# Group norm, shifted-window attention and depthwise convolution on one core: every engine's instructions in written order, softmax split in two, convolution taps written one by one, another prologue

## The chip, the cores and the metric

The kernel runs on one core of a Trainium2 chip. The metric is the device time of one execution in microseconds (us). Three runs of the kernel before gave 5260.55, 5266.62 and 5267.27 us; the median is 5266.62 us. The profile is of a further execution, of 5283.2 us from its first to its last instruction, and all times within the run are read from it.

## The reference

All data are float32. The input x has 16 images of 56 x 56 pixels and 384 channels, and there are two layers with residuals:

```python
x = x + attention(gn(x), w_qkv, w_out, b_out, rel_pos_table)
x = x + depthwise3x3(gn(x), sign(w))      # w clipped, then binarised
```

`gn` normalises each image over 32 groups of 12 channels, so its mean and variance need the whole image. `attention` rolls the image by three rows and columns, cuts it into 8 x 8 windows of 7 x 7 tokens, computes q, k and v (12 heads of 32), a softmax over 49 keys with a position bias and, in the last row and column of windows, a mask, and multiplies by `w_out`. The convolution has nine taps per channel and zero padding. The second `gn` needs all of an image's first layer before the convolution of that image can begin.

## The kernel before

**Tiling.** A strip `s` is one row of eight windows, 7 rows by 56 columns, kept as channels by tokens in three blocks of 128 channels (`NC` = 3); an image has 8 strips (`NS`), the run 128. Half a strip, four windows, is a unit `u`; there are 256. A unit's softmax tile `t` has 128 partitions by 24 rows of 49 scores.

**Loops.** The main loop runs over the units. Each has heavy work on TensorE: an even unit computes the next strip's q and k (`query_key`, six groups of matmuls, L288) and the first third of the previous strip's output (`project`, L401); an odd unit computes the next strip's `value` (four groups, L301), calls `normalize` for the strip after it (ScalarE writes `xn`, L277) and does the other two thirds of `project`. Between them stand `transpose` (three, L358, of the softmaxed scores `e`) and `attend` (L379). At the head of each unit stands `softmax(u + 1)`: the scores (`ps`, L323), then VectorE's scale and bias (L334), maximum (L344), subtraction (L345), ScalarE's `exp` (L347), and VectorE's sum, reciprocal and product (L349, L351, L352).

**Light work.** A table `side` holds other work with due times in units: `fetch` and `load` of the next image (transposes `pl`, L261; ScalarE copy L264; `bn_stats`, L268), the `gn` chain (`norm_gather`, `norm_scale`: statistics to DRAM and back, GpSimd arithmetic, coefficients to DRAM and back, all on GpSimd's DMA queue), `center`, and the convolution of the previous image: `band` (DMA of 16 rows, `xb`), `depthwise` (ScalarE writes the padded, normalised band `hp`, L461, and the centre tap `o`, L475; VectorE adds eight taps, L486) and `store` (transposes `px`, L498; ScalarE copy L499; DMA). An image has four bands of three channel blocks, so twelve depthwise steps, spaced 1.3 units (1.1 for image 14).

**What sets the order.** Only TensorE keeps the order in which the code is written; the other engines are ordered by a scheduler with priorities, which moves the vector part of `softmax` ahead by `SOON`. `issue_after` holds an image's first padded band back until a recent `exp` has been issued.

**Buffers.** All matmul outputs but the scores share a ring of four PSUM banks (`bank`); a new group of matmuls waits until the copy or addition that empties the bank's last use is done. The scores have one buffer of their own. There are two `xb`, two `hp` and five `o` tiles, and eleven strips `x`.

**Before and after the main loop.** The prologue loads and transposes the weights, then the bias table and the depthwise weights, then image 0, strip after strip, with two load buffers `xl`; then its `gn` chain, q and k, and the first scores. After the last unit only the `gn` chain and the convolution of image 15 are left.

Of the kernel before, what the change touches and what calls it, by code (L numbers as in the profile page):

```python
# [33 lines left out]
def kernel(  # L34
# [35 lines left out]
    SOON = 700  # L70
# [6 lines left out]
    xpool = ctx.enter_context(tc.tile_pool(name="x", bufs=11))  # L77
# [7 lines left out]
    hpool = ctx.enter_context(tc.tile_pool(name="hp", bufs=2))  # L85
# [11 lines left out]
    for c in range(NC):  # L97
        nc.scalar.dma_start(bo_sb[:, c : c + 1], b_out[c * P : (c + 1) * P].unsqueeze(1))
    power = const.tile([P, 1], F32, tag="power", name="power")
    nc.gpsimd.memset(power, -0.5)  # L100
# [7 lines left out]
    nc.gpsimd.memset(xn, 0.0)  # L108
    nc.gpsimd.memset(qk[:, :, ST:], 0.0)

    xls = [const.tile([P, NL, C], F32, tag=f"xl{n}", name=f"xl{n}") for n in range(2)]
    for xl in xls:
        nc.gpsimd.memset(xl[:, NL - 1, :], 0.0)

    es = [const.tile([P, NH, 2, HT], F32, tag=f"e{n}", name=f"e{n}") for n in range(2)]
    for e in es:
        nc.gpsimd.memset(e, 0.0)

    def load_weights():
        for dst, src in ((wq_t, w_qkv), (wo_t, w_out)):  # L120
            for r in range(src.shape[0] // P):
                wl = io.tile([P, LG, C], F32, tag="io", name="wl")
                nc.scalar.dma_start(wl[:, 0, :], src[r * P : (r + 1) * P, :])
                pw = bank("pw")
                for c in range(NC):
                    nc.tensor.transpose(pw[:, c * P : (c + 1) * P], wl[:, 0, c * P : (c + 1) * P], ident)
                nc.vector.tensor_copy(
                    dst[:, :, r * P : (r + 1) * P], pw[:, : NC * P].rearrange("p (c q) -> p c q", c=NC)
                )

    def load_depthwise():
        wl = [io.tile([P, LG, C], F32, tag="io", name=f"dwl{n}")[:9, 0, :] for n in range(3)]
        nc.scalar.dma_start(wl[0], w_dw.rearrange("a b c o -> (a b) (c o)"))

        nc.vector.tensor_scalar(wl[1], wl[0], -1.0, 1.0, ALU.max, ALU.min)
        nc.vector.tensor_scalar(wl[0], wl[1], 0.0, None, ALU.is_gt)
        nc.vector.tensor_scalar(wl[2], wl[1], 0.0, None, ALU.is_lt)
        nc.vector.tensor_tensor(wl[0], wl[0], wl[2], ALU.subtract)
        nc.vector.tensor_tensor(wl[0], wl[0], wl[1], ALU.subtract)
        nc.vector.tensor_tensor(wl[0], wl[0], wl[1], ALU.add)  # L140
        pw = bank("pdw")
        for c in range(NC):
            nc.tensor.transpose(pw[:, c * 9 : (c + 1) * 9], wl[0][:, c * P : (c + 1) * P], ident[:9, :9])
        nc.vector.tensor_copy(dw_t, pw[:, : NC * 9].rearrange("p (c t) -> p c t", c=NC))

    def load_bias():

        rel = io.tile([P, LG * C], F32, tag="io", name="rel")[:, : T * NH]
        nc.gpsimd.memset(rel, 0.0)
        flat = rel.rearrange("q (a n) -> q a n", a=WIN)  # L150
        for q in range(T):
            qr, qc = divmod(q, WIN)
            first = (WIN - 1 - qr) * REL + (WIN - 1 - qc)
            row = rel_table[first : first + 1, :]
            src = bass.AP(
                tensor=row.tensor,
                offset=row.offset,
                ap=[[NH, 1], [REL * NH, WIN], [1, WIN * NH]],
            )
            (nc.gpsimd if q % 2 else nc.scalar).dma_start(flat[q : q + 1], src)  # L160
        nc.gpsimd.dma_start(flat[HT : HT + T], flat[0:T])
        mask = io.tile([P, LG * C], F32, tag="io", name="mask")[:, : 2 * T].rearrange("q (v k) -> q v k", v=2)
        nc.gpsimd.memset(mask, 0.0)
        for w in range(2):
            nc.gpsimd.dma_start(mask[w * HT : w * HT + T], wmask[0:T, :, 0:T])
        rel_n = rel.rearrange("q (k j i) -> q i j k", j=NC, i=HPC)
# [13 lines left out]
    def norm_gather(key):  # L180
# [9 lines left out]
        nc.gpsimd.dma_start(by_channel.rearrange("(c p) k -> p c k", p=P), mv)  # L190
        gt = small.tile([GROUPS, GS, 2], F32, tag="gt", name=f"gt{name}")
        nc.gpsimd.dma_start(gt.rearrange("g n k -> g (n k)"), by_channel.rearrange("(g n) k -> g (n k)", n=GS))
        parts[key] = gt

    def norm_scale(key):
# [30 lines left out]
        nc.gpsimd.dma_start(by_channel.rearrange("(g n) k -> g (n k)", n=GS), both.rearrange("g n k -> g (n k)"))  # L226
        coef = small.tile([P, NC, 2], F32, tag="coef", name=f"coef{name}", bufs=4)
        nc.gpsimd.dma_start(coef, by_channel.rearrange("(c p) k -> p c k", p=P))
# [43 lines left out]
    recent = []  # L272
# [39 lines left out]
    def softmax(u):  # L312
# [3 lines left out]
        for j in range(NC):  # L316
            for w in range(2):
                for r in range(2):
                    for i in range(HPC):
# [9 lines left out]
                        )  # L329

        with tc.high_priority(offset=SOON):
            n = NC * 2 * T
            t = two.tile([P, HPC * n], F32, tag="t", name=f"t_{u}", bufs=1)
            nc.vector.scalar_tensor_tensor(  # L334
                t.rearrange("q (i n) -> q i n", i=HPC),
                pp[:, :, :n],
                QSCALE,
                bias[:, int(s % NS == NS - 1)].rearrange("q (i j) w k -> q i (j w k)", i=HPC),
                ALU.mult,
                ALU.add,  # L340
            )
            tr = t.rearrange("q (n k) -> q n k", k=T)
            top = small.tile([P, 2 * NH], F32, tag="top", name=f"top_{u}")
            nc.vector.tensor_reduce(top, tr, AX.X, ALU.max)  # L344
            nc.vector.tensor_tensor(tr, tr, top.unsqueeze(2).to_broadcast([P, 2 * NH, T]), ALU.subtract)  # L345
            e = es[u % 2].rearrange("q h w k -> q (h w) k")[:, :, :T]
            recent[:] = [nc.scalar.activation(e, tr, AF.Exp)]  # L347
            total = small.tile([P, 2 * NH], F32, tag="total", name=f"total_{u}")
            nc.vector.tensor_reduce(total, e, AX.X, ALU.add)  # L349
            inv = small.tile([P, 2 * NH], F32, tag="inv", name=f"inv_{u}")  # L350
            nc.vector.reciprocal(inv, total)  # L351
            nc.vector.tensor_tensor(e, e, inv.unsqueeze(2).to_broadcast([P, 2 * NH, T]), ALU.mult)  # L352
# [99 lines left out]
    def depthwise(b, k, c):  # L452
        coef, cen = coefs[1, b], centers[b]
        xb, rows, at, n = bands.pop((b, k, c))
        hp = hpool.tile([P, BR + 2, W + 2], F32, tag="hp", name=f"hp_{b}_{k}_{c}")
        nc.gpsimd.memset(hp[:, :, 0 : W + 2 : W + 1], 0.0)
# [4 lines left out]
        padded = lambda: nc.scalar.activation(  # L461
# [6 lines left out]
        if k == 0 and c == 0 and recent:  # L468

            with tc.issue_after(recent[0].ins):  # L470
                padded()
        else:
            padded()
# [5 lines left out]
            bias=cen[:, c, 1:2],  # L479
            scale=cen[:, c, 0:1],  # L480
        )
        for t in range(9):
            if t == 4:
                continue
            dy, dx = divmod(t, 3)
            nc.vector.scalar_tensor_tensor(  # L486
                acc, hp[:, dy : dy + BR, dx : dx + W], dw_t[:, c, t : t + 1], acc, ALU.mult, ALU.add
            )
        outs[b, k, c] = acc

# [20 lines left out]
    def plan_conv(p, first, step):  # L511

        at(first, norm_gather, (1, p))
        at(first + 0.7, norm_scale, (1, p))
        at(first + 1.2, center, p)
        for n in range(NB * NC):
            k, c = divmod(n, NC)
            when = first + 1.5 + step * n
            at(max(when - min(step, 1.2), first), band, p, k, c)
            at(when, depthwise, p, k, c)  # L520
        for k in range(NB):
            tiles = -(-BR * W // OT // LG)
            for g in range(tiles):
                at(first + 1.5 + step * NC * (k + 1 + 0.7 * g / tiles) + 0.1, store, p, k, g)

    def plan_load(b):

        for r in range(NS):
            when = NU * (b - 1) + max(1.7 + 1.3 * r, 2 * r - 3)
            at(when - 0.7, fetch, b * NS + r)  # L530
            for c in range(NC):
                at(when + 0.8 * c / NC, load, b * NS + r, c)
        at(when + 0.7, norm_gather, (0, b))
        at(when + 1.5, norm_scale, (0, b))
# [22 lines left out]
    with tc.manual_schedule(engines={mybir.EngineType.PE}):  # L557
        load_weights()
        load_bias()
        load_depthwise()  # L560
        fetch(0)
        for s in range(NS):
            if s + 1 < NS:
                fetch(s + 1)
            for c in range(NC):
                load(s, c)
        norm_gather((0, 0))
        norm_scale((0, 0))
        normalize(0)
        run([(query_key, (0, m)) for m in range(2 * NC)])  # L570
        softmax(0)
        run([(value, (0, n)) for n in range(2 * UPS)])
        normalize(1)
        for b in range(1, B):
            plan_load(b)
            plan_conv(b - 1, NU * b + 1, 1.3 if b < B - 1 else 1.1)
        for u in range(B * NU):
            todo = heavy(u)
            light = [(w, f, a) for w, f, a in sorted(side.pop(u, []), key=lambda i: i[0])]
            if u + 1 < B * NU:  # L580
                softmax(u + 1)
            slots = len(todo)
            n = 0
            for i, (f, args) in enumerate(todo):
                f(*args)
                if i < NC:
                    transpose(u, i)
                elif i == NC:
                    attend(u)
# [3 lines left out]
            for i in range(len(todo), NC + 1):  # L593
                if i < NC:
                    transpose(u, i)
                else:
                    attend(u)
# [3 lines left out]
        recent.clear()  # L601
        plan_conv(B - 1, B * NU, 1.0)
        for u in sorted(side):
            for _, g, a in sorted(side[u], key=lambda i: i[0]):
                g(*a)
# [44 lines left out]
```

## Time and profile before

| stretch of the run | us | what it is |
|---|---|---|
| 0 to 120.6 | 120.6 | prologue, up to the first scores |
| 120.6 to 393 | 272.5 | image 0: attention, loads of image 1, no convolution |
| 14 images (1 to 14) | 315.7 to 320.9 each, mean 317.6 | attention, loads of the next image, convolution of the one before |
| image 15 up to its last scores, 5121.4 | 272 for 7 strips | attention and convolution, no loads |
| 5121.4 to 5283 | 162 | end of attention, `gn` chain, convolution of image 15 |

The stretches are found from the starts of the score matmuls (L323), 96 of which begin each unit. Over the whole span TensorE is busy for 4740.4 us in matmuls, VectorE for 3871.1, ScalarE for 2332.7, GpSimd for 532.4. Some mean durations: a softmax pass of VectorE 1368 to 1383 ns (five for each unit; the scaling with bias is one), the reciprocal 298, a tap 1022, `exp` 1208, an addition into `y` 562 and its statistics 563, a padded band 1116, a centre tap 1054. In these lists a row gives the instruction's line, engine and operation, output and inputs, how often it ran, its busy time and mean, and how long the engine was idle just before it, with what released it.

### The profile page before, as it was taken

How to read it: one execution, taken by the hardware profiler on the slowest of the kernel's cores; microseconds unless marked ns; L12 is line 12 of the kernel's file. 1: busy time of each engine (PE TensorE's matmuls, PEld its weight loads, DVE VectorE, ACT ScalarE, POOL GpSimd, SP SyncE). 2: the span in 40 equal slices, each digit the busy share in tenths (PEclk: the TensorE clock that was granted, in tenths of full speed). 3: DMA queues.
4: the chain of work that ended last, by engine and by line, in shares of the span. 5: the costliest groups of instructions: out<-in, count | busy, mean ns of one | idle time of the engine just before them, and what ended most of it. 6: DMA issues, size and time to landing. Idle time of an engine off the chain costs nothing. (4 is left out here: it accounts for less than half of the span.)

```text
span 5283.2 us, 145019 instructions
## 1 busy us (share of the span) xinstructions
PE 4740.4 (90%) x65127; PEld 3023.6 (57%) x65127; DVE 3871.1 (73%) x4371; ACT 2332.7 (44%) x4417; POOL 532.4 (10%) x1386
## 2 busy tenths in 40 slices
PE   4999989989898998989989899999989999899981
PEld 2665656556565655656556565555656556565551
DVE  2557678777786787778777786777778777787777
ACT  1434435444443544445444444444445444444432
POOL 2001010111101011010111101010010101101000
PEclk9999999999999999999999999999999999999995
DMA  2112212122221212212122221222212122221113
GB/s 66 34 35 55 74 51 81 53 71 71 64 71 53 77 60 68 72 51 80 55 71 68 61 74 55 74 61 70 72 51 77 58 72 68 56 74 51 60 52 91
DMA packets 166078, 337.64 MB, mean 64 GB/s; under 512 B 22304, under 2 KB 124201, under 8 KB 165456
## 3 DMA queue, kind: packets, MB, share of 16 engines
q1 hardware_dynamic: 139008, 244.10, 17.5%
q0 software_dynamic: 23920, 81.82, 4.6%
q8 instruction: 511, 8.37, 0.7%
q10 hardware_dynamic: 2528, 2.44, 0.2%
q14 instruction: 111, 0.91, 0.1%
HBM read 169.69 MB, written 158.47 MB: 62 GB/s over the span
## 5 line engine op out<-in xcount | busy, mean ns | idle before, releaser
L288 PE MATMUL pq<-xn,wq_t 128*128 128x392 f32 x4608 | 1724.0, 515 | 100.4 <-ACT qk L295 77.9
L486 DVE SCALAR_TENSOR_TENSOR o<-hp,dw_t,o 128x784 f32<-128x784 f32 x1536 | 1532.8, 1022 | 293.6 <-ACT o L475 287.5
L288 PEld LDWEIGHTS pq<-xn,wq_t 128*128 128x128 f32 x4608 | 850.1, 196 | 621.5 <-ACT qk L295 88.3
L301 PE MATMUL pv<-wq_t,xn 128*128 128x384 f32 x3072 | 1100.6, 495 | 19.2 <-ACT v L309 16.7
L401 PE MATMUL py<-ot,wo_t 128*128 128x392 f32 x2304 | 832.5, 506 | 18.1 <-ACT v L309 8.7
L295 ACT COPY qk<-pq 128x392 f32<-128x392 f32 x768 | 369.5, 481 | 869.9 <-PE pq L288 869.9
L301 PEld LDWEIGHTS pv<-wq_t,xn 128*128 128x128 f32 x3072 | 543.0, 190 | 309.5 <-ACT v L309 27.4
L409 DVE TENSOR_TENSOR y<-py,x 128x392 f32<-128x392 f32 x384 | 215.8, 562 | 589.0 <-PE py L401 580.5
L401 PEld LDWEIGHTS py<-ot,wo_t 128*128 128x128 f32 x2304 | 430.6, 193 | 311.7 <-issue 15.1
L358 PEld LDWEIGHTS pp<-ident,e 113*128 113x128 f32 x3072 | 371.2, 142 | 258.7 <-issue 155.5
L347 ACT ACTIVATE e<-t 128x1176 f32<-128x1176 f32 x256 | 309.2, 1208 | 452.0 <-DVE t L345 451.8
L349 DVE TENSOR_REDUCE total<-e 128x24 f32<-128x1176 f32 x256 | 352.0, 1375 | 183.8 <-ACT e L347 183.8
L309 ACT COPY v<-pv 128x384 f32<-128x384 f32 x512 | 241.1, 471 | 499.4 <-PE pv L301 499.2
L498 PE MATMUL px<-ident,o 128*112 128x128 f32 x1344 | 225.5, 297 | 249.1 <-ACT qk L295 112.0
L461 ACT ACTIVATE hp<-xb,coef 128x896 f32<-128x896 f32 (+1 forms) x192 | 214.4, 1116 | 505.1 <-POOL coef L437 215.0
L358 PE MATMUL pp<-ident,e 113*128 113x113 f32 x3072 | 429.2, 262 | 3.9 <-DVE e L352 3.3
L334 DVE SCALAR_TENSOR_TENSOR t<-ps,bias 128x1176 f32<-128x1176 f32 x256 | 350.8, 1370 | 93.8 <-PE ps L323 93.8
L364 ACT COPY pt<-pp 128x392 f32<-128x392 f32 x768 | 374.8, 488 | 16.8 <-PE pp L358 16.5
L379 PEld LDWEIGHTS po<-pt,v 49*32 49x32 f32 x24576 | 254.4, 106 | 188.7 <-issue 81.2
L323 PEld LDWEIGHTS ps<-qk 32*64 32x64 f32 x24576 | 282.4, 131 | 136.1 <-issue 86.7
L352 DVE TENSOR_TENSOR e<-e,inv 128x1176 f32<-128x1176 f32 x256 | 353.9, 1383 | 5.7
L345 DVE TENSOR_TENSOR t<-t,top 128x1176 f32<-128x1176 f32 x256 | 352.9, 1379 | 4.7
(73 smaller groups left out, 3653.2 us busy)
## 6 DMA issues: line engine op xcount, KB each, us to landing
mid<-y POOLq DMA_DIRECT2D x112, 619.5 KB, 4.6
out_dram<-xo SPq DMA_DIRECT2D x192, 336.0 KB
xb<-mid SPq DMA_DIRECT2D x96, 472.0 KB
xb<-mid SPq DMA_DIRECT2D x96, 442.5 KB
xl<-in_x_dram SPq DMA_DIRECT2D x112, 288.0 KB
xl<-in_x_dram SPq DMA_DIRECT2D x112, 216.0 KB
out_dram<-xo SPq DMA_DIRECT2D x64, 168.0 KB
xl<-in_x_dram SPq DMA_DIRECT2D x48, 144.0 KB
```

Of the source, the lines that this page charges most:

```text
L288: nc.tensor.matmul(pq[:, :ST].rearrange("p (w t) -> p w t", t=T), wq_t[:, c, m * P : (m + 1) * P], xn[:, c, :, :T], start=(c == 0), stop=( ...
L295: nc.scalar.copy(qk[:, m, :ST], pq[:, :ST])
L301: nc.tensor.matmul(pv[:, :C], xn[:, c, 2 * n : 2 * n + 2].rearrange("p w t -> p (w t)"), wq_t[:, c, 2 * C : 3 * C], start=(c == 0), stop=( ...
L334: nc.vector.scalar_tensor_tensor(t.rearrange("q (i n) -> q i n", i=HPC), pp[:, :, :n], QSCALE, bias[:, int(s % NS == NS - 1)].rearrange("q ...
L345: nc.vector.tensor_tensor(tr, tr, top.unsqueeze(2).to_broadcast([P, 2 * NH, T]), ALU.subtract)
L347: recent[:] = [nc.scalar.activation(e, tr, AF.Exp)]
L349: nc.vector.tensor_reduce(total, e, AX.X, ALU.add)
L352: nc.vector.tensor_tensor(e, e, inv.unsqueeze(2).to_broadcast([P, 2 * NH, T]), ALU.mult)
L358: nc.tensor.transpose(pp[:, i * P : i * P + QT], es[u % 2][:QT, i * NC + j].rearrange("q w k -> q (w k)"), ident[:QT, :QT],)
L364: nc.scalar.copy(pt, pp.rearrange("k (n q) -> k n q", q=HT)[:, :, :T])
L401: nc.tensor.matmul(py[:, :ST], wo_t[:, c, m * P : (m + 1) * P], ots[s][:, c, :], start=(c == 0), stop=(c == NC - 1),)
L486: nc.vector.scalar_tensor_tensor(acc, hp[:, dy : dy + BR, dx : dx + W], dw_t[:, c, t : t + 1], acc, ALU.mult, ALU.add)
```

## The change

Every engine now takes its instructions in written order (`manual_schedule()` without a list of engines), so that the place of each call in the code is its place in the engine's queue. To fit this, `softmax` is split: `scores(u + 1)` with the scaling, maximum and subtraction stays at the head of the unit; the new `softmax(u + 1)`, `exp` and what follows it, is written after the fourth group of heavy work and ahead of `attend`. `depthwise` is split into `pad`, `middle` and eight calls of `tap`, each with its own due time an eighth of a step apart. The `hp` tiles become two fixed ones, zeroed once, so the column memsets go. The convolution starts `lead` = 3 units after the `gn` chain is begun (1.5 before). `plan_load` has new times, and `x` has twelve buffers. The prologue fetches two strips first, stages all weights in `x` buffers, loads image 0, and transposes the weights while the `gn` chain is under way; the bias rows all go on GpSimd's DMA queue. The `gn` chains of image 0 and, after the loop, image 15 use SyncE's DMA queue.

```diff
-    xpool = ctx.enter_context(tc.tile_pool(name="x", bufs=11))
+    xpool = ctx.enter_context(tc.tile_pool(name="x", bufs=12))
...
+    def fetch_weights():
+        rows = [w[r * P : (r + 1) * P, :] for w in (w_qkv, w_out) for r in range(w.shape[0] // P)]
+        for n in range(0, len(rows), NC):
+            wl = xpool.tile([P, NC, ST], F32, tag="x", name=f"wl_{n}")
+            for k in range(NC):
+                nc.scalar.dma_start(wl[:, k, :C], rows[n + k])
...
-            recent[:] = [nc.scalar.activation(e, tr, AF.Exp)]
...
+    def softmax(u):
+        e = es[u % 2].rearrange("q h w k -> q (h w) k")[:, :, :T]
+        nc.scalar.activation(e, shifted.pop(u), AF.Exp)
+        total = small.tile([P, 2 * NH], F32, tag="total", name=f"total_{u}")
+        nc.vector.tensor_reduce(total, e, AX.X, ALU.add)
...
-    def depthwise(b, k, c):
+    def pad(b, k, c):
...
-        nc.gpsimd.memset(hp[:, :, 0 : W + 2 : W + 1], 0.0)
...
+    def tap(b, k, c, t):
+        dy, dx = divmod(t, 3)
+        acc = outs[b, k, c]
+        hp, _ = padded[b, k, c]
+        nc.vector.scalar_tensor_tensor(
+            acc, hp[:, dy : dy + BR, dx : dx + W], dw_t[:, c, t : t + 1], acc, ALU.mult, ALU.add
+        )
...
-            when = first + 1.5 + step * n
-            at(max(when - min(step, 1.2), first), band, p, k, c)
-            at(when, depthwise, p, k, c)
...
+        first += lead
...
+            when = first + step * n
+            at(when - 1.3 * step, band, p, k, c)
+            at(when - 0.65 * step, pad, p, k, c)
+            at(when - 0.45 * step, middle, p, k, c)
+            for i, t in enumerate((0, 1, 2, 3, 5, 6, 7, 8)):
+                at(when + step * i / 8, tap, p, k, c, t)
+            if c == NC - 1:
+                tiles = -(-BR * W // OT // LG)
+                for g in range(tiles):
+                    at(when + step * (1 + 1.5 * g / tiles), store, p, k, g)
...
-            when = NU * (b - 1) + max(1.7 + 1.3 * r, 2 * r - 3)
+            when = NU * (b - 1) + max(1.3 + 1.2 * r, 2 * r - 3.9)
...
-    with tc.manual_schedule(engines={mybir.EngineType.PE}):
+    with tc.manual_schedule():
...
             if u + 1 < B * NU:
-                softmax(u + 1)
+                scores(u + 1)
...
                 elif i == NC:
+                    if u + 1 < B * NU:
+                        softmax(u + 1)
                     attend(u)
...
-        plan_conv(B - 1, B * NU, 1.0)
+        plan_conv(B - 1, B * NU, 1.0, 1.3, nc.sync)
```

## The prediction

> **What bounds the kernel now.** I read the stretches of the run first, each by engine (columns: stretch, length, busy time of each engine with its instructions, granted clock, DMA share, GB/s).
>
> ```profile
> 0.00:120.50 120.50, 41.71 (x171) 30.95 (x171) 28.93 (x62) 17.97 (x33) 27.87 (x68) 1.00 0.31 72
> 120.50:393.00 272.50, 268.61 (x3960) 170.96 (x3960) 152.72 (x164) 112.27 (x223) 12.68 (x34) 1.00 0.13 34
> 1376.00:1693.00 317.00, 295.88 (x4163) 188.61 (x4164) 241.82 (x274) 145.25 (x276) 32.82 (x84) 0.97 0.24 66
> 5121.00:5283.00 162.00, 45.83 (x458) 33.61 (x456) 115.36 (x128) 46.25 (x72) 14.23 (x50) 0.61 0.29 85
> ```
>
> TensorE bounds both image stretches. Image 0, without convolution, is full at full clock: 268.6 of 272.5 us. An image with convolution adds for TensorE only 28 transposed tiles `px` (0.87 us for two, so 12 us): 281 us of work. It takes 317. The missing 36 us are 21 idle (317 - 295.9), about 9.5 of half clock (317 x 0.03), and some 6 of small overlaps lost. VectorE, 242 of 317, has room on average. Prologue and end are bound by chains instead, with TensorE idle. Next I asked who waits for whom.
>
> ```profile
> PE px L498 <- ACT qk L295: 112.0, 22, 11.4
> PE px L498 <- DVE o L486: 106.4, 12, 39.7
> PE pq L288 <- ACT qk L295: 77.9, 44, 3.6
> ...
> ACT hp L461 <- POOL coef L437: 215.0, 15, 23.3
> ...
> ACT x L264 <- DVE y L409: 114.7, 30, 5.9
> ```
>
> TensorE waits for ScalarE to empty a PSUM bank, and ScalarE stands once per image (15 times) behind the first padded band, whose coefficients are not there. One such place, ScalarE's and TensorE's timelines:
>
> ```profile
> 1389.26 0.93 ACT L264 COPY x<-pl 128x392 f32<-128x392 f32 x2
> 1403.17 1.09 ACT L461 ACTIVATE hp<-xb,coef 128x840 f32<-128x840 f32 x1 [12.98 <-POOL coef L437]
> ```
> ```profile
> 1393.64 3.31 PE L288 MATMUL pq<-xn,wq_t 128*128 128x392 f32 x6
> ...
> 1405.61 0.89 PE L498 MATMUL px<-ident,o 128*112 128x128 f32 x3 [5.27 <-ACT qk L295]
> ...
> 1409.12 3.17 PE L288 MATMUL pq<-xn,wq_t 128*128 128x392 f32 x5
> ```
>
> The 13 us on ScalarE leave TensorE 5.3 and 2.7 us without work, and after each the matmuls run slowly (six in 3.31 us; an undisturbed group takes 2.15).
>
> [...]
>
> **The change, part by part.** *The coefficient wait.* With `lead` 3 the first `pad` of an image is written 2.15 units after `norm_gather`, about 38 us at 17.7 us for a unit. The chain took 17.6 us in the prologue (first transfer issued at 87.45, coefficients used at 105.10) and 22 in the contended end; begun some 9 us into its unit, it is ready 7 us or more ahead. GpSimd's row memsets for bands 3 and 0 stand behind it, but the taps that read those rows come later still. So 13 us on ScalarE go, worth 8 idle and about 5 of half clock on TensorE. A twelfth `x` buffer shortens the wait of `x` for `y` (7 us per image on ScalarE), behind which a 3.6 us stop of TensorE stood. Moving the column memsets to the start is free, GpSimd is 10% busy.
>
> *The new waits.* In the changed kernel's order, `exp` stands on ScalarE behind the copy of the fourth heavy group, and on VectorE sum, reciprocal and product stand behind `exp`, with taps behind these. `px` of a band's first tiles is written one to two groups after the band's last tap. With 1.3 units per step the four bands end at 0.6 to 0.9 of an odd unit, after `exp`. From the end of the fourth `value` group: copy from PSUM 0.25 latency (an undisturbed copy starts that much later) + 0.48, `exp` 1.21, sum 1.38, reciprocal 0.30, product 1.38, tap 1.02, about 0.15 of hand-overs: 6.2 us until the last tap is done. In that time TensorE has only `attend`, 1.1 us. Bands 2 and 3: `px` stands right behind `attend`, so TensorE waits 5.1 us, twice. Band 1: one more tap before (1.0), one `project` group (2.1): 4.1. Band 0: in between VectorE has two taps' worth, an addition and two statistics (2.8), TensorE two `project` groups and a load (4.5): 3.5 or more. Sum 17.8 us for each image. Behind a waiting `px` stand `py` and the next unit's scores, so nothing else fills it. In the odd unit without `project` (the second of an image) `middle` and `normalize` (1.05 + 2.2) after `exp` hold q and k up by 2.3. [...]
>
> *An image then:* 281 + 6 + 17.8 + 2.3 + 8.5 = 315.6 against 317.6: 2 us less, 28 for 14 images. In the clean units the order holds: VectorE has 14.6 us of work in an even unit (18.7 long) and 15.7 in an odd one (16), and gives back in the even ones what it loses in waiting for `exp`; softmaxed scores are needed by `transpose` only 3 us into the next unit. Splitting, spreading, and renaming otherwise cost nothing: same instructions.
>
> *Image 15:* step 1.1, no loads. 7 strips at 34.5 and three stops with clock (17) give 259 against 272; VectorE's 7.3 taps per unit take some of it back, which I put at 5: 8 less.
>
> *Prologue.* Now strips wait for weights and bias until 53.5 us and the last strip's statistics end at 87. Changed: weights (2.36 MB) and two strips (1.2 MB) at the 199 GB/s of 4 to 20 us take until 18; three more pairs at 8.7 us (from 53.5 to 80.3 in the trace), 44; transposes and statistics, 46; chain 18, 64; `normalize`, q and k 15.5 as now, 80 for the first scores. Weight transposes (12 copies of 0.56), bias additions (5.1) and 49 bias rows (0.53 each, 26 us on GpSimd) lie beside it. Against 120.6 that is 40.5 less; the first `exp`, now behind four copies and `normalize`, costs 2.5: 38 less. Bounds: chain 14 to 20, pairs 6 (at 199 GB/s) to 9.5: 30 to 48.
>
> *End.* The chain no longer stands behind two stores of `mid` (first hop 7.8 us against 5.1 in the prologue, second 4.0 against 2.6): 4 less. Image 14's last nine taps fall into the chain's wait: 2. The 93 us of taps stay. 6 less, 2 to 10.
>
> Sum: 5266.6 - 28 - 8 - 38 - 6 = **5187**.
>
> **The rivals.** *The waits for taps are short.* If TensorE is itself late at these places, or stores fall where VectorE is done, half of the waits and of their clock go: 281 + 6 + 10 + 4 = 301, 16.6 less per image (232), 15 for image 15, with 44 at the ends: 4976. For it: VectorE has 75 us free per image. Against: `exp` is tied to TensorE's fourth group, so VectorE's lead doesn't help. *VectorE becomes the bound.* Each unit's subtraction ends at about 5.5 us, three taps later it is 8.6, and `exp` ends at 12.3. If VectorE, late otherwise, can't use that gap and some 1.3 us of waiting for `py`, an image needs 242 + 16 x 5 = 322: 62 more over 14, 4 more in image 15, 44 less at the ends: 5289, slower. For it: before, VectorE could take any ready tap; now each waiting instruction holds all behind it. Against: lateness itself fills the gap.
>
> **How the numbers follow.** 5187 has a chance of 0.57; its spread (waits 15 to 22 us per image,[...] prologue bounds) is 60 either way. 4976 has 0.23, 5289 has 0.20, each about 40 either way. Faster by over 0.2% (below 5256): 0.53 + 0.23 + 0.01 = 0.77; within: 0.03 + 0.03 = 0.06; slower: 0.01 + 0.16 = 0.17. The range 5000 to 5290 leaves out about 0.12 below and 0.08 above.
>
> **What would show it.** Right: no wait of `hp` for `coef` but at the end; `px` waiting for `o` some 64 times at 3 to 5 us; first scores at about 80 us; 316 us per image with a clock near 0.97. Wrong: `px` hardly waiting and images near 300; ScalarE or TensorE waiting for VectorE's subtraction or `y` in every unit; a chain of coefficients that arrives after its `pad`; a prologue still above 95 us.

## The result, and the profile after

The changed kernel takes 5089.91 us (median of four runs, 5086.96 to 5103.28), the kernel before 5264.39 beside it: a ratio of 0.9674, 95% interval 0.9655 to 0.9693. The change was forecast to gain 80 us and gains 174. The direction held and the time lies in the forecast range, but the forecast gain was less than half of the measured one.

The profiled execution of before took 5284.97 us, 18 us more than the median in front of the prediction; that of the changed kernel, 5088.51, about 1 us less than its own median. So the parts in the table add up to 197 us and not to 174. In which part those 22 us sit can't be told from one profile; up to 3 of them may be in the prologue, since the kernels of experiments 4 and 5, which have the prologue of before, reached their first scores at 118.3 and 117.9 us. Image 0 is counted from the head of its first unit, which stands 9.1 us behind the first scores in both kernels, so that it ends where image 1 begins.

| stretch | before | after | difference | forecast |
|---|---|---|---|---|
| up to the first scores | 120.6 | 79.2 | -41.4 | -38 (with 2.5 for the first `exp`) |
| image 0, from its first unit | 273.2 | 274.3 | +1.1 | in the line above |
| images 1 to 14 | 4446.6 | 4302.0 | -144.6 | -28 |
| image 15, 7 strips | 271.9 | 256.4 | -15.5 | -8 |
| last scores to the end | 161.8 | 165.5 | +3.7 | -6 |

The same stretches of the changed kernel by engine; the third row is image 9, whose length, 307.2 us, six other late images share to 0.1 us:

```profile
0.00:79.20 79.20, 38.13 (x171) 29.34 (x171) 26.30 (x58) 19.90 (x37) 40.56 (x87) 0.94 0.48 110
79.20:362.60 283.40, 279.07 (x4087) 177.40 (x4086) 154.79 (x168) 117.33 (x233) 12.45 (x34) 0.99 0.12 32
...
2821.50:3128.70 307.20, 290.74 (x4071) 187.16 (x4070) 246.46 (x271) 146.83 (x276) 32.03 (x72) 0.97 0.24 68
...
4921.00:5086.50 165.50, 49.64 (x469) 36.39 (x468) 137.60 (x143) 50.07 (x81) 11.01 (x38) 0.61 0.30 92
```

TensorE is idle for 16.5 us of the image, where it had been for 21 of the image that the prediction shows. Who waits for whom on TensorE in this image:

```profile
PE px L518 <- DVE o L507: 14.8, 4, 4.4
PE pq L306 <- ACT xn L295: 1.2, 1, 1.2
PE pl L279 <- issue: 0.2, 1, 0.2
```

Over the whole run, TensorE's first row of waits, and ScalarE's only row in which a padded band waits for its coefficients (total, times, longest):

```profile
PE px L518 <- DVE o L507: 307.2, 72, 10.5
```
```profile
ACT hp L482 <- POOL coef L455: 27.0, 1, 27.0
```

The row of before had 15 such waits: 14 in images, of 13.7 us on average, and one of 23.3 at the end. Those in the images have gone, and the one at the end is left. In their place TensorE waits, four times in an image, for the last tap of a band (59 of the row's 72 waits; the other 13, of 93.9 us, stand behind the last scores). The timeline of one such place:

```profile
2887.63 1.09 PE L397 MATMUL po<-pt,v 49*32 49x49 f32 x96
2887.73 0.48 ACT L327 COPY v<-pv 128x384 f32<-128x384 f32 x1 [0.47 <-PE pv L319]
2888.11 1.21 ACT L365 ACTIVATE e<-t 128x1176 f32<-128x1176 f32 x1
2888.65 0.43 PE L518 MATMUL px<-ident,o 128*112 128x128 f32 x2
...
2889.35 1.38 DVE L367 TENSOR_REDUCE total<-e 128x24 f32<-128x1176 f32 x1 [3.01 <-ACT e L365]
...
2891.10 1.39 DVE L370 TENSOR_TENSOR e<-e,inv 128x1176 f32<-128x1176 f32 x1
2892.40 1.03 DVE L507 SCALAR_TENSOR_TENSOR o<-hp,dw_t,o 128x784 f32<-128x784 f32 x1
2893.48 1.10 PE L518 MATMUL px<-ident,o 128*112 128x128 f32 x4 [4.40 <-DVE o L507]
```

The copy of the fourth `value` group, `exp`, sum, reciprocal, product, tap: VectorE stood idle for 3.0 us in the middle of it, since its order let it take nothing else, and TensorE for 4.4.

### The profile page after: what moved, and what is told of

Same layout as the page of the kernel before. It is cut to its first block, busy times and chain, and to the rows that moved or that the text cites. A ratio compares the mean times of both kernels' runs of the same rounds, so it can differ in the third digit from the quotient of the medians.

```text
span 5086.5 us, 144410 instructions
## 1 busy us (share of the span) xinstructions
PE 4682.5 (92%) x65127; PEld 3016.6 (59%) x65127; DVE 3965.5 (78%) x4367; ACT 2356.2 (46%) x4421; POOL 529.5 (10%) x1213
## 4 chain that ended last, share of the span: by engine, by line
PE 81%; DVE 13%; ACT 4%; DMA 1%; issue 1%; POOL 0%; SPq 0%; ACTq 0%; DVEq 0%; POOLq 0%
PE pq L306 30%; PE pv L319 20%; PE py L419 12%; PE pp L376 6%; DVE o L507 5%; PE ps L341 5%; PE po L397 3%; PE px L518 3%; DVE total L367 2%; DVE e L370 2%; PE pl L279 2%; ACT e L365 2%; ACT v L327 1%; DVE y L427 1%; DMA xl<-in_x_dram 1%
## 5 line engine op out<-in xcount | busy, mean ns | idle before, releaser
L306 PE MATMUL pq<-xn,wq_t 128*128 128x392 f32 x4608 | 1686.3, 504 | 22.7 <-ACT xn L295 19.4
L507 DVE SCALAR_TENSOR_TENSOR o<-hp,dw_t,o 128x784 f32<-128x784 f32 x1536 | 1571.6, 1027 | 31.9 <-ACT o L494 10.7
L306 PEld LDWEIGHTS pq<-xn,wq_t 128*128 128x128 f32 x4608 | 824.9, 191 | 511.0 <-ACT xn L295 26.1
L419 PE MATMUL py<-ot,wo_t 128*128 128x392 f32 x2304 | 875.0, 527 | 1.5 <-ACT ot L406 1.1
L419 PEld LDWEIGHTS py<-ot,wo_t 128*128 128x128 f32 x2304 | 454.0, 204 | 305.5 <-issue 56.7
L518 PE MATMUL px<-ident,o 128*112 128x128 f32 x1344 | 226.7, 300 | 316.8 <-DVE o L507 307.2
L439 POOL COPY y<-y 128x63 f32<-128x63 f32 x128 | 32.2, 252 | 3511.5 <-DVE y L427 3511.4
L518 PEld LDWEIGHTS px<-ident,o 128*112 128x112 f32 x1344 | 166.2, 145 | 367.6 <-DVE o L507 304.5
L359 DVE TENSOR_REDUCE top<-t 128x24 f32<-128x1176 f32 x256 | 352.8, 1378 | 8.8
```

Of the source, the lines that this page charges most:

```text
L306: nc.tensor.matmul(pq[:, :ST].rearrange("p (w t) -> p w t", t=T), wq_t[:, c, m * P : (m + 1) * P], xn[:, c, :, :T], start=(c == 0), stop=( ...
L419: nc.tensor.matmul(py[:, :ST], wo_t[:, c, m * P : (m + 1) * P], ots[s][:, c, :], start=(c == 0), stop=(c == NC - 1),)
L507: nc.vector.scalar_tensor_tensor(acc, hp[:, dy : dy + BR, dx : dx + W], dw_t[:, c, t : t + 1], acc, ALU.mult, ALU.add)
L518: nc.tensor.transpose(po[:OT, c * P : (c + 1) * P], flat[c][:, t * OT : (t + 1) * OT], ident)
```

## The experiments

Theory A at the outset: the middle gains because the coefficients are there before the first padded band, and loses to the waits for taps. Theory B: the written order itself is the gain, or VectorE the bound. "Images" are lengths of the late, settled ones (8 to 14) where nothing else is said.

**1. The convolution begun one unit after its chain.** In `plan_conv`:

```diff
-            at(when - 1.3 * step, band, p, k, c)
-            at(when - 0.65 * step, pad, p, k, c)
-            at(when - 0.45 * step, middle, p, k, c)
+            at(max(when - 1.3 * step, first - lead + 0.05), band, p, k, c)
+            at(max(when - 0.65 * step, first - lead + 0.25), pad, p, k, c)
+            at(max(when - 0.45 * step, first - lead + 0.3), middle, p, k, c)
...
-            plan_conv(b - 1, NU * b + 1, 1.3 if b < B - 1 else 1.1, 3, nc.gpsimd)
+            plan_conv(b - 1, NU * b + 1, 1.3 if b < B - 1 else 1.1, 1, nc.gpsimd)
```

> The changed kernel, with the convolution of an image begun 1 unit after its group-norm chain instead of 3 (first band, pad and centre tap no earlier than 0.05, 0.25 and 0.3 units after the chain's start); all else, with the parity of the units, stays. Theory A, that the middle of the run gains by the coefficients being there before the first padded band: ScalarE waits again for the coefficients, 20 to 25 us in each of 15 images, TensorE loses some 15 us and clock, images go from 307 to about 325 us, the run to about 5330. Theory B, that the gain is in the order of the engines and not in the lead: images within 3 us of 307, the run within 50 of 5090.

Measured: 5327.0 us, 1.3% slower than the kernel before (ratio 1.0129, 1.0099 to 1.0158); images 2 to 14 take 320 to 328. The waits of TensorE and ScalarE in one image:

```profile
PE po L397 <- ACT x L282: 17.7, 1, 17.7
PE px L518 <- DVE o L507: 10.4, 3, 4.4
```
```profile
ACT hp L482 <- POOL coef L455: 20.3, 1, 20.3
```

ScalarE stands for 20 us, and TensorE, once the ring of four PSUM banks is full, for 17.7. The wait is longer than in the kernel before, where the scheduler placed the band one `exp` later than it stands here. With the same order and everything else alike, the lead alone decides over 237 us.

**2. Stores a third of a step later.**

```diff
-                    at(when + step * (1 + 1.5 * g / tiles), store, p, k, g)
+                    at(when + step * (1.35 + 1.3 * g / tiles), store, p, k, g)
```

> The changed kernel, with each band's stores written 0.35 of a step (0.45 units, about 8 us) later, the last of a band's four only 0.2 later. Theory A, that TensorE stands at px for the band's last tap (14.8 us an image): these waits fall below 3 us an image, the slow clock windows from 17 us to below 6, images from 307 to about 287, the run to about 4800. Theory B, that VectorE is the bound behind these waits: they turn up at other instructions (y, e, scores), images stay above 300, the run above 4990.

Measured: 4793.02 us (ratio to the kernel before 0.9114, 0.9087 to 0.914), images 285 (287 on average from image 2 to 14). An image by engine, and all of TensorE's waits in it:

```profile
3239.60:3524.30 284.70, 283.12 (x4069) 183.35 (x4068) 245.66 (x272) 145.85 (x276) 31.93 (x72) 1.00 0.26 74
```
```profile
PE pq L306 <- ACT xn L295: 1.2, 1, 1.2
```

The four waits are gone, nothing took their place, and the granted clock is 1.00. So the 14.8 us of waits cost 22.5 us an image with the slow windows that went with them. VectorE, busy for 246 of 285, is not the bound: theory B's second half falls.

**3. The changed code under the scheduler.**

```diff
-    with tc.manual_schedule():
+    with tc.manual_schedule(engines={mybir.EngineType.PE}):
```

> The changed kernel, with only TensorE in written order and the other engines left to the scheduler as before (without the old priority of the softmax). Theory A, that lead and prologue make the gain and the fixed order only carries it: no wait for coefficients, first scores within 5 us of 79, images 300 to 312, the run within 80 of 5090. Theory B, that the written order of ScalarE and VectorE is what gains: images above 315, the run above 5200.

Measured: 5193.33 us, first scores at 82.7, images 314. Neither theory's numbers: the prologue's gain stays, but in spite of `lead` 3 ScalarE waits for the coefficients once in an image (the changed code has no `issue_after` any more, so nothing holds the padded band here):

```profile
ACT hp L482 <- POOL coef L455: 12.7, 1, 12.7
```

**4. The kernel before, with the lead alone.**

```diff
-            when = first + 1.5 + step * n
+            when = first + 3 + step * n
...
-                at(first + 1.5 + step * NC * (k + 1 + 0.7 * g / tiles) + 0.1, store, p, k, g)
+                at(first + 3 + step * NC * (k + 1 + 0.7 * g / tiles) + 0.1, store, p, k, g)
```

> The kernel before, with its convolution begun 3 units after the group-norm chain instead of 1.5, and nothing else. Theory A: ScalarE's wait of 13 us per image for the coefficients goes, images from 317.6 to about 303, the run from 5264 to about 5060. Theory B: the wait goes or stays, images stay within 4 us of 317, the run above 5210.

Measured: 5241.99 us, 0.4% less than before (ratio 0.9964, 0.9953 to 0.9974), images 313 to 318. A miss for theory A. The row of ScalarE's waits in one image shows why:

```profile
ACT o L475 <- POOL cen L440: 10.7, 1, 10.7
```

The padded band, which `issue_after` holds back, now comes in time; the centre tap of the same band, which nothing holds, waits for its own coefficients instead. In the trace the first padded band stands one `exp` later than before in images 1 to 14, and the centre tap no later at all. Theory C: under the scheduler a due time binds no single instruction; one left free is placed ahead of its data.

**5. The same, with the centre tap held as well.**

```diff
-        nc.scalar.activation(
+        centre = lambda: nc.scalar.activation(
...
+        if k == 0 and c == 0 and recent:
+            with tc.issue_after(recent[0].ins):
+                centre()
+        else:
+            centre()
```

> The kernel before, with the convolution begun at 3 units as in e4_before_lead3, and with an image's first centre tap held back behind the same exp as its first padded band. In e4 the wait for the coefficients had moved from the padded band to this centre tap, which the scheduler had placed ahead (172 us in 15 images). Theory C, that the scheduler's place for single ScalarE instructions, not the due time, decides: with both held the wait goes, images from 315 to about 305 us, the run to about 5100. Rival: the scheduler puts another instruction in the way, or TensorE's waits come from its order at large: the run stays above 5200.

Measured: 5105.62 us (5087.94 and 5123.29; ratio 0.9703, 0.9621 to 0.9784), images 1 to 14 take 303 to 312, with no wait of ScalarE for GpSimd in an image of the profile (3176 to 3480 us). One held instruction more than in experiment 4 gains 136 us (119 to 154, as its two runs lie 35 us apart). From the first to the last scores this kernel's profile, of its longer run, has 4841.1 us and the changed kernel's 4841.7: two edits under the scheduler make all of the change's gain there. Theory C stands, and in this comparison the written order adds nothing on balance in the middle; it is one way to fix the place of every instruction, these two among them. No kernel here came to the 285 us of experiment 2 under the scheduler; whether one could was not tried.

**6. The last image's taps in turn from two blocks,** on top of experiment 2.

```diff
-        hp = hps[count[0] % 2]
+        hp = hps[count[0] % 3]
...
-                at(when + step * i / 8, tap, p, k, c, t)
+                at(when + over * step * i / 8, tap, p, k, c, t)
...
-        plan_conv(B - 1, B * NU, 1.0, 1.3, nc.sync)
+        plan_conv(B - 1, B * NU, 1.0, 1.3, nc.sync, 2)
```

> The kernel of e2_store_late, with the taps of the last image's convolution (behind the main loop) taken in turn from two channel blocks instead of eight in a row into the same tile; three padded tiles instead of two, its stores right behind the taps. Theory: a tap that adds into the tile of the tap just before it waits for that tap's end, and one that doesn't starts earlier (pitch 1.07 us in the changed kernel's tail, 0.95 to 0.97 in the kernel before, where the scheduler took two blocks in turn): the 96 taps take about 93 us instead of 102, the run 4785 against 4793. Rival: the pitch has another cause (what GpSimd or the DMA do): no change, 4793.

Measured: 4783.25 us (4782.31 and 4784.18; ratio 0.909, 0.9064 to 0.9117), the fastest kernel here. VectorE at the end of the run, before, after, and in this kernel (start, length, and how many taps):

```profile
5180.70 93.03 DVE L486 SCALAR_TENSOR_TENSOR o<-hp,dw_t,o 128x784 f32<-128x784 f32 x96 [25.91 <-ACT o L475]
```
```profile
4975.85 101.59 DVE L507 SCALAR_TENSOR_TENSOR o<-hp,dw_t,o 128x784 f32<-128x784 f32 x96 [10.74 <-ACT o L494]
```
```profile
4678.21 93.21 DVE L507 SCALAR_TENSOR_TENSOR o<-hp,dw_t,o 128x784 f32<-128x784 f32 x96 [10.71 <-ACT o L494]
```

Taken in turn, the taps are back at their old speed. The stretch behind the last scores fell from 167.9 (experiment 2) to 159.8; the first scores also came 3.2 us earlier in this profile, which is no more than the prologue's scatter (experiment 9).

**7. `exp` one group earlier.**

```diff
                 if i < NC:
                     transpose(u, i)
+                    if i == NC - 1 and u + 1 < B * NU:
+                        softmax(u + 1)
                 elif i == NC:
-                    if u + 1 < B * NU:
-                        softmax(u + 1)
                     attend(u)
```

> The changed kernel, with the second half of the softmax written after the third group of heavy work and its transpose instead of after the fourth. Theory A, that exp behind the fourth group's copy sets the time of the band's last tap: exp comes 2 us earlier, the four px waits of an image shrink from 14.8 to about 7 us, with less slow clock; images from 307 to about 296, the run to about 4940. Rival: exp then waits for the subtraction on VectorE and holds ScalarE's copies up: images stay at 307 or above, the run at 5090 or more.

Measured: 4992.0 us, images 300. In one image the four waits are 10.5 us instead of 14.8, the longest 3.6 instead of 4.4. The direction is theory A's, the size a half to two thirds of it. At all four places VectorE still stands idle for `exp` (1.65 to 2.11 us), so `exp` does set the tap's time, and no backlog of VectorE's does. But at two of the places (bands 1 and 2) one tap more than in the changed kernel now stands between the softmax product and `px`. Band 1, VectorE in this kernel, then the taps of the same place in the changed one:

```profile
3289.90 1.38 DVE L367 TENSOR_REDUCE total<-e 128x24 f32<-128x1176 f32 x1 [2.11 <-ACT e L365]
...
3292.98 3.16 DVE L507 SCALAR_TENSOR_TENSOR o<-hp,dw_t,o 128x784 f32<-128x784 f32 x3
```
```profile
3048.18 2.10 DVE L507 SCALAR_TENSOR_TENSOR o<-hp,dw_t,o 128x784 f32<-128x784 f32 x2
```

At band 3, where no tap was added, TensorE's wait shrank by 1.9 us (4.4 to 2.5), at bands 1 and 2 by 0.8.

**8. The eight taps of a block together,** on top of experiment 2.

```diff
-                at(when + step * i / 8, tap, p, k, c, t)
+                at(when, tap, p, k, c, t)
```

> The kernel of e2_store_late, with the eight taps of a block written together where the first one stands, not an eighth of a step apart. Theory A: eight taps in a row (8.5 us) make VectorE late once in 1.3 units; y, exp and softmaxed scores come some 5 us too late for TensorE at some of these places: images from 285 to about 291, the run to about 4880. Rival: VectorE's slack takes it, spreading is not needed: within 20 us of 4793.

Measured: 5041.22 us, images 304: 248 us slower than experiment 2, where theory A expected some 90 and its rival nothing. TensorE in one image:

```profile
PE pp L376 <- DVE e L370: 8.8, 2, 8.4
PE pq L306 <- DVE y L427: 2.1, 2, 1.6
PE px L518 <- DVE y L427: 2.1, 1, 2.1
PE pq L306 <- ACT ot L406: 1.7, 1, 1.7
```

Spreading the taps is needed: with eight in a row the softmaxed scores come up to 8.4 us late.

**9. The weights' transposes ahead of image 0's strips again,** in the changed kernel.

```diff
+        for n in range(NC + 1):
+            load_weights(n)
+        load_depthwise()
+        add_bias()
         for s in range(NS):
...
-        for n in range(NC + 1):
-            load_weights(n)
-        load_depthwise()
-        add_bias()
```

> The changed kernel, with the weights' transposes, the depthwise weights and the bias additions written ahead of image 0's strips again, as in the kernel before; the early fetches and the staging stay. Theory: the prologue gains by loading image 0 beside weights and bias: the strips wait for them again until some 40 to 45 us, then 35 us for strips, 18 for the chain and 16 to the first scores: these at about 110 instead of 79, the run at about 5120. Rival: the DMA's rate alone sets the prologue: first scores within 6 us of 79, the run at 5090.

Measured: 5108.68 us, first scores at 96.2, between the two theories. The time of the whole run decides nothing here: the kernel before took 5281.09 us beside it, and the ratio is 0.9673, as good as the changed kernel's 0.9674. The prologue's own trace does. The strips waited only until 20.0 us and not 40 to 45 (the bias rows are no longer in ScalarE's queue ahead of the depthwise weights, for which TensorE had waited), but VectorE's statistics stood behind the bias additions, and these waited for the mask:

```profile
49.00 5.20 DVE L188 TENSOR_TENSOR bias<-rel,mask 128x147 f32<-128x147 f32 x16 [28.71 <-DMA mask<-in_wmask_dram]
...
54.13 11.31 DVE L286 BATCH_NORM_STATS2 st<-x 128x6 f32<-128x392 f32 x24
```

The chain began at 66.2 instead of 49.7. So of the 41 us that the prologue gains, 17 are the place of this work and the other 24 are the rest of the rewrite (early fetches, staged weights, bias rows off ScalarE's queue), which was not taken apart. Either figure is good to some 3 us: the same prologue ended between 79.2 and 81.9 in the changed kernel and experiments 1, 2, 7 and 8.

## Why the prediction was right and wrong

**Right: the bound, the wait that goes, the wait that comes.** TensorE bounds the images; the coefficient wait leaves and `px` waits for the last taps, four times in an image, along the chain that the prediction added up. Brought back in experiment 1, longer than it had been (20.3 us in the image shown), the first wait costs 237 us; the second gains 297 when experiment 2 takes it out. What the first was worth in the kernel before, experiment 5 tells best: 317.7 to 307.5 us for an image (mean of images 2 to 14), 10 us where the prediction had 13.

**Right by luck: the length of the slow clock.** The 8.5 us of the forecast sum, for 17 us at half clock behind five stops, were the author's estimate, as was the clock's share in the sums for image 15 and for the rival with short waits. The image shown has 17.1 us at half clock (granted clock 0.50), but as 6.8, 3.4 and 6.8 us, at three of four stops. 3.0 of them fell while TensorE stood anyway, so that they cost 7.0 us and not 8.5.

**Wrong: the sum for an image,** "281 + 6 + 17.8 + 2.3 + 8.5". It gives 315.6, and 307.2 were measured: 283.7 of work, 16.5 of stops, 7.0 of half clock. These 8 us over 14 images, with an image 1 of 296 us whose convolution starts late, are the miss. Three terms were mis-sized besides the clock's.

*TensorE's own work,* "281 + 6", was carried over unchanged on the ground that the instructions are the same. Counted at full clock (busy time, less half of its part in half-clock windows) it is 283.7 us in the image shown, 3.3 less. 287 was right for the kernel before (287.3, mean of images 2 to 14), but the 6 were not "small overlaps lost". The stretch of image 0 from which the 281 came ends 10 us before image 0 does, and its first units have no earlier strip to project, so it holds 30 `py` matmuls fewer and 12 `pv` more than an image with convolution, which has 144 and 192. The rows of the two stretches (the second takes in one `py` of a neighbour):

```profile
L301 PE MATMUL pv<-wq_t,xn 128*128 128x384 f32 x204 | 72.5, 494 | 0.5 <-ACT v L309 0.5
L401 PE MATMUL py<-ot,wo_t 128*128 128x392 f32 x114 | 40.6, 498 | 0.7 <-DVE y L409 0.7
```
```profile
L301 PE MATMUL pv<-wq_t,xn 128*128 128x384 f32 x192 | 68.8, 495 | 1.0 <-ACT v L309 0.9
L401 PE MATMUL py<-ot,wo_t 128*128 128x392 f32 x145 | 53.0, 510 | 1.1 <-ACT xo L499 0.6 <-ACT v L309 0.5
```

At 0.34 us each (18 `py` in 6.08 us at 1052.70 in the kernel before) the 18 more are 6 us, an estimate. The fall from 287.3 does not go with the length of the stops: the mean is 283.7 in the changed kernel, 283.1 in experiment 1 with 30 us idle in an image and 283.3 in experiment 2 with 3. Most of it goes with the written order: the same code under the scheduler, experiment 3, has 286.4. Why TensorE needs less in the written order stays open.

*The four waits*, 17.8 forecast, are 14.8: 4.4, 4.4, 3.4 and 2.5 for 5.1, 5.1, 4.1 and 3.5. The timeline above shows two causes. Two of the three transposes of a `px` tile read blocks that are long done and run ahead of the wait (0.43 us). And the copy does not start 0.25 us behind the group's last matmul, as the prediction read it, but 0.04 (2887.69 to 2887.73; the median of undisturbed copies in the kernel before is the same), so that the chain took 5.8 us and not 6.2.

*The 2.3 us* for `normalize` are 1.2.

**Wrong: the end.** 6 less forecast, 3.7 more measured. The chain itself did as said and better: from the first transfer to the first padded band 17.1 us (4956.63 to 4973.72) against 22.5 (5156.17 to 5178.64). What failed is "the 93 us of taps stay": written eight in a row, they take 101.6. The 2 us for image 14's taps did not come either: the stretch ahead of the chain is 0.9 us longer (35.7 for 34.8).

**Image 15:** 15.5 less, 8 forecast; the 5 us that I gave VectorE's denser taps did not come.

**Prologue:** first scores at 79.2, forecast 80. The strips' statistics ended at 48.8 (46 forecast), the chain on SyncE's queue took 15.2 us (49.67 to 64.89) and not 18, so that two misses cancelled.

**The rivals.** VectorE as the bound is refuted by experiment 2. "The waits for taps are short" was not the case: they are 14.8 us an image where it had 10. The measured 5090 lies between its 4976 and the 5187 forecast for the other reasons named.

## What to carry to other kernels

When a fixed order is written, each first use of a late result is a place where its engine can stop with everything behind it, as TensorE did here for 14.8 us an image: put it by the time at which the result is there, which the trace gives, and put a consumer on the bounding engine one more wait's length behind its producer; here moving four stores by 8 us was worth 297 us, more than the whole rewrite. Before giving a schedule up for a written one, look which single instructions the scheduler puts ahead of their data; here holding two gave the same in the middle of the run. Before calling what a sum leaves over a loss, count the instructions of the two stretches that are compared; here 6 us of "small overlaps" were matmuls that one of them did not have.

## What the runs showed of the hardware

A VectorE tap that adds into the tile of the tap just before it started 1.07 us after that one, and one that follows a tap of another tile 0.95 us after it (medians of the last 96 taps: 1.071 in the changed kernel and experiment 2, 0.946 in the kernel before and experiment 6). In the changed kernel's tail the 11 short steps among the 95 are those from one block to the next. Per tap of 784 elements, in-place chains took 13% more here than two such chains in turn (1.071 for 0.946 us). An in-place tap started 0.04 us after the end of the one before, the other kind 0.08 us ahead of it. Where these 0.12 us come from was not shown.

In the image shown, the half clock (granted clock 0.50) set in within the two stops of TensorE of 4.4 us and lasted 6.8 us each time; it set in 1.4 us after the stop of 2.5 us and lasted 3.4; at the stop of 3.4 us it did not. The length of a stop alone does not decide it: of the changed kernel's stops from 700 to 4800 us, all 27 of 4.4 us had the half clock set in within them or in the 4 us behind, 12 of 14 of 2.5 us, but only 4 of 13 of 3.4 us. At the place of the kernel before that the prediction shows, it set in 1.3 us after the stop of 2.7 us and lasted 3.4 (from 1394.67), and within the stop of 5.3 us and lasted 6.8 (from 1404.91). In all, the 14.8 us that went in experiment 2 took 7.7 us more with them.
